# Decoder and gated cross attention on one core: mixing moved to the head of the step that begins another batch's scores, with new step lists for the products

## The chip, the cores and the metric

The kernel runs on one core of a Trainium2 chip. A core has five engines with queues of their own: TensorE (PE in the profile, its weight loads PEld), VectorE (DVE), ScalarE (ACT), GpSimd (POOL) and SyncE (SP), which here only issues DMAs. Each works through its instructions in order; semaphores hold an instruction until what it needs is there. The metric is the time of one execution in device microseconds (us). Lower is better.

## What is computed

Sixteen batches of 128 tokens with 512 features go through a decoder layer (self attention, cross attention, MLP) and then through a gated cross attention. All is float32. The reference, cut to what matters:

```python
# attention, 16 heads of 32
scores = einsum('bhqd,bhkd->bhqk', q, k) / sqrt(32)
scores = scores * mask - 10000.0 * (1.0 - mask)
probs = softmax(scores, axis=-1)
ctx = einsum('bhqk,bhkd->bhqd', probs, v)

# decoder layer
ln = layernorm(x, ln1_s, ln1_b)
q, k, v = split(ln @ w_qkv + b_qkv, 3)
x = x + merge_heads(attention(q, k, v, ltor_mask)) @ w_ao + b_ao
q = layernorm(x, ln2_s, ln2_b) @ w_q + b_q
k, v = split(ctx_2048 @ w_kv + b_kv, 2)
x = x + merge_heads(attention(q, k, v, cross_mask)) @ w_co + b_co
x = x + gelu(layernorm(x, ln3_s, ln3_b) @ w1 + b1) @ w2 + b2

# gated cross attention
a = layernorm(ctx_2048, ln_gamma, ln_beta)
Q, K, V = x @ Wq.T, a @ Wk.T, a @ Wv.T
out = x + tanh(gate) * (merge_heads(attention(Q, K, V, mask)) @ Wo.T)
```

## The kernel before

**Sections.** The sixteen batches form four groups of four. A *section* is the attention of one group: A0 to A3 (self attention), B0 to B3 (cross attention) and D0 to D3 (gated). `attend` (line 662) runs a list of sections twice: once the eight of the decoder, then, after the MLP, the four gated ones. Each call of it is a *run*. The MLP lies between the runs and is not touched.

**Steps.** A section has 16 steps, four for each batch. `step(k, ...)` (line 677) counts `k` on through the whole run, and `m = k % 4` is the place within a batch. The 16 heads of a batch are worked on as four *units* of four heads; a unit belongs to one step. What a unit goes through is spread over several steps: scaled (or, in D, masked with its least value found) on VectorE in the batch's first three steps (`SCALED`, line 658), exponentials on ScalarE a step later (`exp_unit`, four instructions), normalized on POOL after that (`norm_unit`, with a reciprocal of the sums on VectorE), turned by a 32x32 transpose on VectorE and sent to DRAM at `k - 3` (`turn_unit`, tiles `s` to `away`). Two units form a pair, which comes back from DRAM in four DMAs, with rows and columns of the big blocks exchanged (`receive_pair`, line 598, tile `pT`, three buffers).

**Scores and mixing.** At `m == 0`, `scores` (line 523) issues 16 small matmuls on the head's 32 rows (32x128 of the array, tile `sc`, four PSUM banks, which the next batch's scores use again). `mix` (line 609) multiplies the returned probabilities with the values: 16 small matmuls into 32 columns each (128x32 of the array, tile `av`). Its result is evicted by `mixed_out` on ScalarE into `mT` (one buffer), and `out_project` (line 644) makes four full matmuls of it (tile `mo`), whose sum goes to `x` on VectorE (`finish`). In the gated run the last product is put off: for D0 and D1 `put_away` sends `mT` to DRAM, for D2 it stays in SBUF, and these projections are done in D3 as block products (`added_product`, tile `mm_o`). The last batch of the gated run (`by_array`) is turned by TensorE instead of by DMA. Every matmul shows as two records in the trace.

**Where mixing stood.** In step `k`, batch `k // 4 - 2` was mixed at `m == 2`, that is at step `4b + 10` for batch `b`; its pairs were received at the head of steps `4b + 6` and `4b + 8`, and its output product came at `4b + 12`, at `m == 0`, after that step's jobs.

**Products.** While a section's attention runs, the projections of the next one are made between its steps. Most are block products with seven instead of eight quarter products (`block_product`, line 384, jobs 1 to 7, four matmuls each, eight records of 128x256). Jobs 1, 6 and 7 add up in the same PSUM bank `mm0`, which ScalarE copies out after each; 5 and 3 share `mm1` in the same way, with adds on VectorE; 2 and 4 take a bank of tag `pt` (two buffers), which `av` and `mo` also use. Which job comes in which step stands in lists written out by hand: `BLOCKS`, `SECOND_BLOCKS`, `CROSS_BLOCKS`, `GATED_BLOCKS` and `DEFERRED_BLOCKS` (lines 465 to 494); each is one dictionary per product, step to jobs. `blocks_plan` (line 496) joins them; without `as_listed` it puts jobs 1, 6 and 7 of a step first. The queries of B are made by whole chunks (`query_chunk`, 512 wide), not by blocks. The sums of operands that the blocks need are made on POOL in listed steps.

**Order in time.** The program's order of instructions on each engine is the order of issue. `afterwards` (line 79) puts something off to the call of `due` (line 82) in the next step, so that TensorE's result is there when ScalarE or VectorE comes to it. In a step the order is: receive a pair, scores, `due`, the jobs, output product, mixing, preparing the section after next (`ahead.prepare`), turning a unit, normalizing and exponentials, scaling.

## Time and profile before

| | |
|---|---|
| median of 3 runs | 1166.22 us (1162.94 to 1170.1) |
| profiled execution | 1168.78 us |
| its span, first to last instruction | 1167.0 us, 22047 instructions |
| mean granted TensorE clock | 0.994 |
| DMA | 259.80 MB, mean 223 GB/s |

The run of the decoder takes the first 560 us or so of the span, the MLP follows to 945, and the gated run takes the rest. A step of the A and B sections lasts 3.8 us on average: the scores of A2's first batch start at 162.82 us and those of A3's at 223.96, 16 steps later.

All instructions are recorded by one helper, so all carry its line, L50; they are told apart by engine and tile. `sc_A` are the scores of A, `av_B` the mixing of B, `mm_k_D` a key product of D. A row of the timeline gives start, busy time, engine, tiles, shape and count, and in brackets how long the engine had been idle before and what ended the wait. The costliest of the instructions that the change moves, or that stand beside them, by their mean durations:

| instruction | engine | ns |
|---|---|---|
| exponentials of one head block, 128x128, four a unit | ACT | 393 |
| normalizing a unit, 128x512 | POOL | 1041 |
| adding the mask in A, 128x512 | POOL | 1280 |
| mask and least value in D, 128x128, four a unit | DVE | 283 |
| eviction of `av` in A and B, 128x128, four a batch | ACT | 357 |
| eviction of `av` in D, 128x512 | ACT | 568 |
| scaling a unit in A, 128x512 | DVE | 681 |

### The profile page before, as it was taken

How to read it: one execution, taken by the hardware profiler on the slowest of the kernel's cores; microseconds unless marked ns; L12 is line 12 of the kernel's file. 1: busy time of each engine (PE TensorE's matmuls, PEld its weight loads, DVE VectorE, ACT ScalarE, POOL GpSimd, SP SyncE). 2: the span in 40 equal slices, each digit the busy share in tenths (PEclk: the TensorE clock that was granted, in tenths of full speed). 3: DMA queues.
4: the chain of work that ended last, by engine and by line, in shares of the span. 5: the costliest groups of instructions: out<-in, count | busy, mean ns of one | idle time of the engine just before them, and what ended most of it. 6: DMA issues, size and time to landing. Idle time of an engine off the chain costs nothing. (4 is left out here: it accounts for less than half of the span.)

```text
span 1167.0 us, 22047 instructions
## 1 busy us (share of the span) xinstructions
PE 1134.5 (97%) x7210; PEld 868.3 (74%) x7210; DVE 739.2 (63%) x1894; ACT 605.6 (52%) x2132; POOL 701.5 (60%) x636
## 2 busy tenths in 40 slices
PE   7999999999999999998999999999999999999988
PEld 5877777657575757545788888888888777878866
DVE  7678878797878877876663633543432247767753
ACT  2467667666666766674221333232222247867653
POOL 7698878688868776684333424433341367545973
PEclk9999999999999999999999999999999999999989
DMA  6598979999889879898796696696457728988964
GB/s 227 148 221 220 240 188 222 248 235 267 199 229 208 239 202 255 243 290 252 264 287 235 188 273 197 193 301 224 154 184 249 211 48 229 249 215 251 264 191 163
DMA packets 325266, 259.80 MB, mean 223 GB/s; under 512 B 83544, under 2 KB 280608, under 8 KB 320288
## 3 DMA queue, kind: packets, MB, share of 16 engines
q1 hardware_dynamic: 325112, 258.38, 78.0%
q8 instruction: 58, 0.95, 0.3%
q14 instruction: 56, 0.46, 0.1%
q10 hardware_dynamic: 40, 0.01, 0.0%
HBM read 163.94 MB, written 94.37 MB: 221 GB/s over the span
## 5 line engine op out<-in xcount | busy, mean ns | idle before, releaser
L50 ACT ACTIVATE s_A<-s_A,mn_A 128x128 f32<-128x128 f32 x256 | 99.5, 393 | 51.5 <-issue 37.3
L50 DVE TENSOR_TENSOR h<-h,h 128x512 f32<-128x512 f32 x80 | 54.9, 686 | 112.6 <-PE h L50 112.6
L50 ACT ACTIVATE s_B<-s_B,mn_B 128x128 f32<-128x128 f32 x256 | 99.5, 393 | 46.6 <-issue 32.5
L50 ACT ACTIVATE h<-h 128x512 f32<-128x512 f32 x64 | 40.3, 630 | 160.6 <-DVE h L50 160.6
L50 POOL TENSOR_TENSOR s_D<-s_D,sum_D 128x512 f32<-128x512 f32 x64 | 66.5, 1040 | 67.8 <-DVE sum_D L50 66.3
L50 ACT ACTIVATE s_D<-s_D,mn_D 128x128 f32<-128x128 f32 x256 | 99.2, 392 | 0.4 <-issue 0.4
L50 POOL TENSOR_TENSOR s_B<-s_B,sum_B 128x512 f32<-128x512 f32 x64 | 66.8, 1045 | 48.7 <-DVE sum_B L50 44.3
L50 POOL TENSOR_TENSOR s_A<-s_A,sum_A 128x512 f32<-128x512 f32 x64 | 66.6, 1041 | 36.0 <-DVE sum_A L50 35.3
L50 POOL TENSOR_TENSOR s_A<-s_A,ma 128x512 f32<-128x512 f32 x64 | 81.9, 1280 | 5.4 <-DVE s_A L50 3.7
L50 POOL TENSOR_TENSOR s_B<-s_B,mask 128x512 f32<-128x512 f32 x64 | 81.3, 1270 | 2.1 <-DMA away_B<-s_B 0.4
L50 POOL TENSOR_TENSOR rstd_aD<-rstd_aD,mhalf 128x1 f32<-128x1 f32 x12 | 6.6, 548 | 114.6 <-DVE rstd_aD L50 101.1
L50 POOL TENSOR_TENSOR sh<-h 128x512 f32<-128x512 f32 x32 | 40.7, 1272 | 50.9 <-ACT h L50 43.0
L50 PE MATMUL mo_B<-w_co,mT_B 128*128 128x512 f32 x128 | 60.5, 616 | 2.1 <-ACT mT_B L50 2.1
L50 PE MATMUL h<-T_C,t 128*128 128x256 f32 x256 | 60.7, 380 | 1.4 <-DVE h L50 1.4
L50 PE MATMUL h<-T_C,w 128*128 128x256 f32 x256 | 61.0, 381 | 0.8 <-DVE h L50 0.8
L50 PE MATMUL h<-sx,t 128*128 128x256 f32 x256 | 60.6, 380 | 0.0
L50 PE MATMUL o<-w,h 128*128 128x256 f32 x256 | 60.5, 379 | 0.0
L50 PE MATMUL o<-t,h 128*128 128x256 f32 x256 | 60.5, 379 | 0.0
L50 PE MATMUL o<-t,sh 128*128 128x256 f32 x256 | 60.5, 379 | 0.0
L50 PE MATMUL mo_A<-w_ao,mT_A 128*128 128x512 f32 x128 | 59.1, 604 | 0.0
L50 DVE CUSTOM_DVE_ANT_0 s_D<-sc_D,gmask 128x128 f32<-128x128 f32 x256 | 57.2, 283 | 0.9 <-DMA turned_x<-x_D 0.9
L50 PE MATMUL mm_q_B<-T_B,w_cq 128*128 128x512 f32 x128 | 57.3, 595 | 0.0
(324 smaller groups left out, 2986.1 us busy)
## 6 DMA issues: line engine op xcount, KB each, us to landing
t<-kept SPq DMA_DIRECT2D x24, 1024.0 KB, 6.9
away_A<-s_A SPq DMA_DIRECT2D x64, 256.0 KB, 3.0
pT_A<-away_A SPq DMA_DIRECT2D x128, 128.0 KB, 3.0
away_B<-s_B SPq DMA_DIRECT2D x64, 256.0 KB, 5.2
pT_B<-away_B SPq DMA_DIRECT2D x128, 128.0 KB, 3.6
away_D<-s_D SPq DMA_DIRECT2D x60, 256.0 KB, 3.7
pT_D<-away_D SPq DMA_DIRECT2D x120, 128.0 KB, 2.8
w<-in_L_xattn_w_dram SPq DMA_DIRECT2D x24, 512.0 KB, 5.6
```

The costliest lines, as they stand in the source:

```text
L50: return lambda *args, **kw: self.tc.keep_in_program_order(call(*args, **kw))
```

## The change

Mixing of batch `b` goes from step `4b + 10` to the head of step `4b + 12`, ahead of the scores of batch `b + 3`; its eviction is issued in the same step after `due`, and its output product (or the sending of `mT`) follows two steps after the mixing. The receives go two steps later too, to steps `4b + 8` and `4b + 10`, and now stand behind the scores in the step. Batches whose mixing would fall later than twelve steps before the scores of the run's last batch, that is behind the first step of the run's last section, keep their old steps (`k - 2`, `at - 2`), and the last batch of the gated run keeps its own. The lists of jobs are written anew, `blocks_plan` takes every list in the order in which it is written, B0 gets a list of its own (`FIRST_CROSS_BLOCKS`), the query chunks of B begin one step earlier, and the sums for B's value weights too.

```diff
--- before.py
+++ after.py
@@ -463,9 +463,9 @@
         return [[t[:, 2 * j : 2 * j + 2, i * HF : (i + 1) * HF] for j in range(2)] for i in range(2)]
 
     BLOCKS = (
-        {1: (1, 2), 2: (6,), 3: (7, 5), 5: (4,), 6: (3,)},
-        {5: (1,), 6: (2,), 7: (6,), 9: (7, 5), 10: (4,), 13: (3,)},
-        {10: (1,), 11: (6, 2), 13: (7,), 14: (5,), 15: (4, 3)},
+        {0: (1,), 1: (2, 6), 2: (5,), 3: (7, 4), 5: (3,)},
+        {4: (1,), 5: (2,), 7: (6, 5), 8: (7,), 9: (4,), 11: (3,)},
+        {9: (1,), 11: (2,), 12: (6,), 13: (5, 7), 15: (4, 3)},
     )
 
     FIRST_BLOCKS = (
@@ -474,31 +474,32 @@
     )
     SECOND_BLOCKS = (
         {4: (1, 2), 5: (6, 5), 6: (7, 4), 8: (3,)},
-        {7: (1, 2), 8: (6,), 9: (7, 5), 10: (4,), 11: (3,)},
-        {12: (1,), 13: (6, 2), 14: (7, 5), 15: (4, 3)},
+        {7: (1, 2), 8: (6,), 9: (5, 7), 10: (4,), 11: (3,)},
+        {10: (1,), 11: (2,), 12: (6,), 13: (5, 7), 15: (4, 3)},
     )
 
     CROSS_BLOCKS = (
-        {6: (1,), 7: (6, 2), 9: (7, 5), 10: (4,), 11: (3,)},
-        {11: (1,), 13: (6, 2), 14: (7, 5), 15: (4, 3)},
+        {4: (1,), 7: (2, 6), 8: (5,), 9: (7, 4), 11: (3,)},
+        {10: (1,), 11: (2,), 12: (6,), 13: (5, 7), 15: (4, 3)},
     )
+    FIRST_CROSS_BLOCKS = {6: (1,), 7: (2, 6), 8: (5,), 9: (7, 4), 11: (3,)}, CROSS_BLOCKS[1]
     GATED_BLOCKS = (
-        {0: (1,), 1: (2, 6), 2: (5, 7), 3: (4,), 5: (3,)},
-        {5: (1,), 6: (2, 6), 7: (7,), 8: (5,), 9: (4,), 10: (3,)},
-        {11: (1, 2), 12: (6,), 13: (5, 7), 14: (4,), 15: (3,)},
+        {0: (1,), 1: (2, 6), 2: (5,), 3: (7, 4), 5: (3,)},
+        {4: (1,), 5: (2,), 6: (6,), 7: (5, 7), 8: (4,), 9: (3,)},
+        {9: (1,), 10: (2,), 11: (6, 5), 13: (7, 4), 15: (3,)},
     )
     DEFERRED_BLOCKS = (
         {0: (1,), 1: (2, 6), 2: (5, 7), 3: (4,), 5: (3,)},
         {5: (1,), 6: (2, 6), 7: (5, 7), 8: (4,), 10: (3,)},
-        {12: (1,), 13: (2, 6), 14: (5, 7), 15: (4,), 17: (3,)},
+        {9: (1,), 11: (2, 6), 13: (5, 7), 15: (4,), 17: (3,)},
     )
 
-    def blocks_plan(products, blocks, as_listed=False):
+    def blocks_plan(products, blocks):
         out = {}
         for jobs, steps_ in zip(products, blocks):
             for step, ns in steps_.items():
-                out.setdefault(step, []).extend((not as_listed and n not in (1, 6, 7), jobs[n]) for n in ns)
-        return [([job for _, job in sorted(jobs, key=lambda j: j[0])], [step] * len(jobs)) for step, jobs in out.items()]
+                out.setdefault(step, []).extend(jobs[n] for n in ns)
+        return [(jobs, [step] * len(jobs)) for step, jobs in out.items()]
 
 
 
@@ -616,7 +617,8 @@
                     av[j * HD : (j + 1) * HD, c * S : (c + 1) * S], sec.v[:, b, h * HD : (h + 1) * HD],
                     bt.pT[j][:, :, c, :], start=True, stop=True,
                 )
-        mT = work.tile([P, KC, S], F32, tag="s", name=f"mT_{bt.name}", bufs=7) if bt.by_array else sec.mixed_tile(b)
+        at_end = work.tile([P, KC, S], F32, tag="s", name=f"mT_{bt.name}", bufs=7) if bt.by_array else None
+        mT = bt.mT = sec.mixed_tile(b) if at_end is None else at_end
 
         def mixed_out():
             if sec.v_bias is None:
@@ -627,8 +629,7 @@
                         mT[:, c], av[:, c * S : (c + 1) * S], AF.Identity, bias=col(sec.v_bias[0], sec.v_bias[1] + c)
                     )
 
-        afterwards("act", mixed_out)
-        bt.mT = mT
+        return mixed_out
 
     def out_project_last(bt):
 
@@ -670,40 +671,59 @@
         units, batches = [], []
         projected = deque()
 
+        last = (len(sections) * GB - 1) * GB
+
         def by_transfer(n):
 
-            return min(n, (len(sections) * GB - 1) * GB) if ready else n
+            return min(n, last) if ready else n
+
+        mixed_at, received_at = {}, {}
+        for b in range(len(sections) * GB):
+            k, at = (b + 3) * GB, (b + 2) * GB
+            if k > last - 3 * GB:
+                k, at = k - 2, at - 2
+            if ready and b * GB == last:
+                k = last + 7
+            else:
+                for half in range(2):
+                    received_at.setdefault(at + 2 * half, []).append(b * GB + 2 * half + 1)
+            mixed_at[k] = b
 
         def step(k, bt=None, jobs=(), ahead=None):
 
             m = k % GB
-            pair = k - 5
-            if pair % 2 and 0 <= pair < by_transfer(len(units)):
-                receive_pair(*units[pair])
+            pairs, done = received_at.get(k, []), mixed_at.get(k)
+            beside_scores = done is not None and m == 0
+            if beside_scores:
+                mixed_out = mix(batches[done])
             if m == 0 and bt is not None:
                 scores(bt)
+            for pair in pairs:
+                receive_pair(*units[pair])
             due()
+            if beside_scores:
+                mixed_out()
+                projected.append((k, batches[done]))
             for job in jobs:
                 job()
-            last_mix = ready and k == by_transfer(k) + 7
+            last_mix = ready and k == last + 7
             if last_mix:
-                mix(batches[-1])
-                projected.append(batches[-1])
-            if projected and (m == 0 or ready and bt is None):
-                before = projected.popleft()
+                afterwards("act", mix(batches[-1]))
+                projected.append((k, batches[-1]))
+            if projected and k - projected[0][0] >= (1 if ready and bt is None else 2):
+                before = projected.popleft()[1]
                 if before.by_array:
                     out_project_last(before)
                 elif before.sec.deferred:
                     afterwards("act", lambda: before.sec.put_away(before))
                 else:
                     out_project(before)
-            done = k // GB - 2
-            first_turned = ready and k == by_transfer(k) + 6
+            first_turned = ready and k == last + 6
             if first_turned:
                 turn_by_array(*units[k - 3])
-            if m == 2 and 0 <= done < len(batches) - ready:
-                mix(batches[done])
-                projected.append(batches[done])
+            if done is not None and not (beside_scores or last_mix):
+                afterwards("act", mix(batches[done]))
+                projected.append((k, batches[done]))
             if ahead is not None:
                 ahead.prepare(k % NS)
             if 0 <= k - 3 < len(units) and not first_turned:
@@ -727,8 +747,7 @@
 
         k = 0
         for i, sec in enumerate(sections):
-            last = i + 1 == len(sections)
-            jobs = others() if last else sections[i + 1].jobs()
+            jobs = others() if i + 1 == len(sections) else sections[i + 1].jobs()
             ahead = sections[i + 2] if i + 2 < len(sections) else after if i + 2 == len(sections) else None
             for b in range(GB):
                 bt = Batch(sec, b)
@@ -938,8 +957,8 @@
                 block_product(by_quarters(self.v), self.v_sides, token_sides, True, f"v_{n}"),
             ]
             return plan(
-                ([lambda c=c: self.query_chunk(c) for c in range(KC)], [1, 2, 3, 5]),
-                *blocks_plan(products, CROSS_BLOCKS), ([lambda: mask_terms(self.ms, self.ma)], [7]),
+                ([lambda c=c: self.query_chunk(c) for c in range(KC)], [0, 1, 3, 5]),
+                *blocks_plan(products, CROSS_BLOCKS if g else FIRST_CROSS_BLOCKS), ([lambda: mask_terms(self.ms, self.ma)], [7]),
                 ([lambda o=o: nc.gpsimd.tensor_tensor(*o) for o in sums], [0, 1, 2, 3]),
                 *(self.weights_begin() if g == 0 else decoder[NG + g - 1].tokens_again([5, 9, 13])),
             )
@@ -979,7 +998,7 @@
 
             return (
                 late_weights(), ([lambda n=n: k_sum(n) for n in range(4)], [4, 4, 5, 5]),
-                ([lambda n=n: v_sum(n) for n in range(4)], [9, 10, 11, 12]),
+                ([lambda n=n: v_sum(n) for n in range(4)], [8, 9, 10, 11]),
             )
 
         def scale_mask(self, s, sc, b):
@@ -1517,7 +1536,7 @@
             elif g == 3:
                 more = self.deferred_start()
             return plan(
-                *blocks_plan(products, GATED_BLOCKS, True), ([by_pool(o) for o in a_sums], [0, 1, 2, 3]), ([mask], [9]), *more
+                *blocks_plan(products, GATED_BLOCKS), ([by_pool(o) for o in a_sums], [0, 1, 2, 3]), ([mask], [9]), *more
             )
 
         def deferred_start(self):
@@ -1570,7 +1589,7 @@
             return (
                 ([lambda n=n: fetch_part("x0", x[0], n) for n in range(2, GB)], [1, 1]),
                 ([lambda g=g: add_later(g) for g in (1, 2) for _ in range(4)], [0, 1, 2, 3, 8, 9, 9, 10]),
-                *blocks_plan(later, DEFERRED_BLOCKS, True),
+                *blocks_plan(later, DEFERRED_BLOCKS),
                 ([lambda g=g, b=b: send(g, b) for g in range(3) for b in range(GB)], [8, 9, 10, 11, 13, 14, 15, 16, 19, 19, 19, 19]),
             )
```

## The prediction

> **What bounds the kernel now.** I read the page's busy table and clock row first, then the TensorE timeline, the waits, and the windows by section.
>
> ```profile
> PE 1134.5 (97%) x7210; PEld 868.3 (74%) x7210; DVE 739.2 (63%) x1894; ACT 605.6 (52%) x2132; POOL 701.5 (60%) x636
> PEclk9999999999999999999999999999999999999989
> ```
>
> TensorE is the bound: the others have a third or more of the span free. It is idle for 1167.0 - 1134.5 = 32.5 us, but busy time also hides lost time, so I took start-to-start times from its timeline (start, busy us, work):
>
> ```profile
> 385.75 3.62 PE L50 MATMUL mm_k_B<-x,w_ck 128*128 128x256 f32 x16
> 389.30 1.08 PE L50 MATMUL av_B<-pT_B,v_B 128*32 128x128 f32 x32
> 390.31 1.99 PE L50 MATMUL mm_v_B<-w_cv,T_e 128*128 128x256 f32 x8
> 392.14 1.89 PE L50 MATMUL mm_k_B<-T_e,sums_c 128*128 128x256 f32 x8
> 393.96 1.17 PE L50 MATMUL sc_B<-k_B,q_B 32*128 32x128 f32 x32
> 395.06 3.70 PE L50 MATMUL mo_B<-w_co,mT_B 128*128 128x512 f32 x8
> ```
>
> A block product (8 records of 128x256) in a run of its kind takes 1.73 us (400.32 to 402.05 in the same timeline). The two here take 1.83 (just after the mixing, av) and 1.82 (just before the scores, sc): each entry into small matmuls costs 0.10 us and each exit 0.10. A batch enters and leaves twice, for av and for sc.
>
> ```profile
> 1123.40 1.08 PE L50 MATMUL av_D<-pT_D,v_D 128*32 128x128 f32 x32
> 1124.41 0.49 PE L50 MATMUL sc_D<-k_D,q_D 32*128 32x128 f32 x4
> 1125.11 0.45 PE L50 MATMUL sc_D<-k_D,q_D 32*128 32x128 f32 x2 [0.21 <-DVE mn_D L50]
> 1128.72 2.04 PE L50 MATMUL sc_D<-k_D,q_D 32*128 32x128 f32 x26 [3.16 <-DVE mn_D L50]
> 1130.69 3.78 PE L50 MATMUL mm_o_D<-w_go,mT_D 128*128 128x256 f32 x8
> ```
>
> This is the only place where av is followed directly by sc: sc starts 1.01 us after av, as a full-array product does. It also shows the largest stall: the last batch's scores wait for VectorE to free their banks (6.28 us from 1124.41 to 1130.69 instead of the usual 1.10), and the next product then runs at half speed (3.58 us to its successor instead of 1.73).
>
> ```profile
> 1026.34 0.41 PE L50 MATMUL av_D<-pT_D,v_D 128*32 128x128 f32 x4
> 1029.48 1.92 PE L50 MATMUL av_D<-pT_D,v_D 128*32 128x128 f32 x28 [2.73 <-DMA pT_D<-away_D]
> 1031.33 3.99 PE L50 MATMUL mm_v_D<-w_gv,T_a 128*128 128x256 f32 x15
> ```
>
> Here the mixing waits for its transposed probabilities, which come back from DRAM. av takes 4.99 us instead of 1.01, and the product behind it 4.14 instead of 3.45: 4.67 us lost. The windows of the second and third gated section:
>
> ```profile
> 995.28:1046.61 51.33, 48.51 (x425) 39.87 (x424) 34.56 (x175) 37.30 (x153) 26.61 (x25) 0.97 0.90 239
> 1046.61:1092.91 46.30, 46.30 (x426) 38.44 (x425) 34.67 (x175) 33.98 (x150) 30.66 (x28) 1.00 0.88 248
> ```
>
> Same work, 5 us apart (first number length, second TensorE busy): D1 stalls, D2 does not.
>
> **The change part by part.** No instruction is added or removed; matmuls, evictions and DMAs keep their number.
>
> *Switches.* Mixing goes to the head of a step that opens with scores, for batches 0 to 25 of the decoder run and 0 to 9 of the gated run: 36. Each loses one exit and one entry: 0.107 + 0.096 = 0.203 us by the rows above, 36 x 0.203 = 7.3 us. Bounds: 0, if the drain only moves, to 7.3; I take 7.3, because the row at 1124.41 is the very sequence and shows no extra cost. [...]
>
> *Stalls in A and B.* At 153.56 and 214.69 a value product waits for VectorE's add of the key product 3 one step before, in the same bank (2.68 us instead of 1.73): 0.95 each. The new lists put 3 at step 11 and value 5 at 13, so both go: 1.9. At 250.09 and 436.39 product 6 waits for ScalarE's copy of product 1 from bank mm0 (1.2 each). With 1 at step 4 and 6 at 7 the second goes; in the first section of B, 1 stays at step 6 and the cover is product 2 (1.73) in place of av (1.0), so about 0.8 goes. Together 3.9, bounds 0 to 4.3. The moved jobs meet this: product 6 of A's queries comes at step 1 and needs POOL's second sum, done at 164.95 for a step 0 that begins at 162.82; TensorE reaches it 5.7 us into that section, so it is covered. ScalarE's eviction of av (four times 0.36) now stands at the step's head, behind it the copy of the step's product and four exponentials (1.56); the output product that needs it follows two steps later, 7 us, so it costs nothing.
>
> *Gated sections.* Stalls of D0 and D1, from start-to-start times: 965.93 0.84, 970.42 1.35, 978.46 1.02, 1016.44 0.49, 1026.34 4.67: 8.4 us. The receives of the probabilities go two steps later as the mixing does, so SP no longer waits for the send just before them. What is left is issue and landing:
>
> ```profile
> 1022.33 2.63 SPq L50 DMA_DIRECT2D pT_D<-away_D  x4
> pT_D<-away_D SPq DMA_DIRECT2D x120, 128.0 KB, 2.8
> ```
>
> Undisturbed, four issues take 1.75 us and land 2.8 later: 4.55. But the second pair is now asked for at the third step of a batch, and TensorE has only steps 2 and 3 until av: three products, 5.2 us, and at a section's end (steps 14 and 15) one product, 1.73, where before sc and three products (6.4) stood between. In A and B an output product stands there too: 6.9 or more, covered. In D the first three batches of a section just hold. At the end VectorE (mask 1.14, transpose 0.70 per unit) sets SP's time: transpose of step 13 about 4.0 us after step 12 begins, receive at 4.4, landed at 9.0, TensorE there at 7.5: a wait of 1.5 at three section ends, 4.5 us. ScalarE's exponentials and its group copies (0.8) end in time for the next scores, barely. Between no wait and 4.67 for each of ten batches I take 4.5, nearer to D2's row, which has none. One SP wait is new: the fetch of D1's kept mixing at step 11 stands in the same step as its last write (3.5 to land); the next receive is a step later with two steps to spare. Net 8.4 - 4.5 = 3.9.
>
> [...]
>
> *End.* The third deferred product set begins at step 9 instead of 12: products 1, 2 and 6 (3 x 1.73 = 5.2 us) now stand before the last batch's scores and fill its 5.18 us stall; the slow clock behind it (1.85 + 0.24) goes too: 7.3. In return two copies on ScalarE (0.58 each), an add on VectorE (0.69) and one on POOL (1.27) come into the chain that held those scores: I leave 1.5 as wait. After the scores TensorE had no gap until 1163.85, while VectorE waited 3.90 us and ScalarE 6.94 for it, so the others can follow a tail that is shorter by three products. Gain 5.8, bounds 0 to 7.3. The stalls at the end of the decoder run (523 to 552, some 9 us) stay: there the mixing is where it was.
>
> *Sum:* 7.3 + 3.9 + 3.9 + 5.8 = 20.9. The profiled execution took 1168.78 (span 1167.0); less 20.9 that is 1147.9. It lies 2.6 above the median 1166.22, from which the sum gives 1145.3. I say 1147.
>
> **The rivals.** *(a) The gated sections give back what they got:* each of their ten batches waits about 1.5 us instead of three, 15 us; net -6.6 there, gain 7.3 + 3.9 - 6.6 + 5.8 = 10.4, 1158. For: the cover fell from 8 to 10 us to 5.2; against: SP no longer waits for the sends (34.7 us of its waits). *(b) Slower:* the landing comes later than the cover in all ten gated batches, and each wait slows the clock as at 1026.34: 10 x 4.67 = 46.7 against 7.3 + 3.9 + 5.8 + 8.4 = 25.4, net +21, about 1189. It decides from 2.5 us per batch upward. For: DMA queues are 88 to 90% busy in D; against: landings there have a median of 2.8. *(c) It does not do what it says:* switching between the two small forms costs what it saves, and every filled stall comes back at the next bank; only the 3.9 of A and B remains, 1164.
>
> **How the numbers follow.** Forecast 0.66, (a) 0.16, (b) 0.09, (c) 0.09. A measurement of this kernel tells about 1% from no change: below 1154.6 is faster, above 1177.9 slower. (a) and (c) lie within 1%, except a fifth of (a): faster 0.69, same 0.22, slower 0.09. The forecast's best end is all stalls gone, 7.3 + 4.3 + 8.4 + 7.3 = 27.3, from the median 1139; I put the low end at 1138. Upward the range takes in (a) and most of (c): 1163.
>
> **What would show it.** Right: av followed by sc 1.01 us later in 36 places; A's sections at 59.4 instead of 61.1; no wait for DVE near the last scores; the tail after them near 26 us instead of 33. Wrong: waits of av_D for the DMA of pT_D over 4.5 us in total, or a new granted clock below 0.95 between 960 and 1120; waits of sc_D for DVE at the first step of a gated section.

## The result and the profile after

The changed kernel is a little slower: 1169.45 us against 1165.38 in the same comparison (22 runs of each), ratio 1.0033, 95% interval 1.0022 to 1.0043. A second comparison (run after_again) gave 1.0024, 1.0011 to 1.0036. The prediction said 1147 us, 1138 to 1163.

The page of the profiled execution (span 1167.4 us) looks like that of before; three microseconds less of busy TensorE, and slow clock in an earlier slice:

```profile
PE 1131.5 (97%) x7210; PEld 870.0 (75%) x7210; DVE 738.8 (63%) x1894; ACT 608.2 (52%) x2132; POOL 700.1 (60%) x636
PEclk9999999999999999999999999999999999999899
```

The TensorE timeline around the place shown before (start, busy us, work) now has the pair:

```profile
433.93 1.89 PE L50 MATMUL mm_k_B<-x,sums_c 128*128 128x256 f32 x8
435.75 1.08 PE L50 MATMUL av_B<-pT_B,v_B 128*32 128x128 f32 x32
436.76 1.17 PE L50 MATMUL sc_B<-k_B,q_B 32*128 32x128 f32 x32
437.87 1.99 PE L50 MATMUL mm_k_B<-x,w_ck 128*128 128x256 f32 x8
```

The scores start 1.01 us after the mixing, and there is one entry (433.93 to 435.75 is 1.82) and one exit (437.87 to 439.70 is 1.83). The pair stands so in 36 places, 27 of them at 1.01 or 1.02; in the other nine the mixing waits. The tail is as forecast too; the last scores (1135.75) wait for nobody:

```profile
1132.10 1.99 PE L50 MATMUL mm_o_D<-w_go,mT_D 128*128 128x256 f32 x8
1133.93 1.89 PE L50 MATMUL mm_o_D<-gsums_o,sums_mT 128*128 128x256 f32 x8
1135.75 1.17 PE L50 MATMUL sc_D<-k_D,q_D 32*128 32x128 f32 x32
1136.85 3.70 PE L50 MATMUL mo_D<-w_go,mT_D 128*128 128x512 f32 x8
```

So the saved switches and the shorter tail are there. Starts of scores in the two traces tell where they went:

| stretch | before | after | difference | forecast |
|---|---|---|---|---|
| to the first scores (A0) | 39.73 | 41.18 | +1.5 | 0 |
| A0 to the last decoder section (B3) | 433.39 | 427.07 | -6.3 | -9.2 (26 x 0.203, and 3.9) |
| B3, MLP, to D0 | 474.76 | 478.56 | +3.8 | 0 |
| D0 to D3 | 145.03 | 151.21 | +6.2 | -5.9 (10 x 0.203, and 3.9) |
| D3 to the end of the span | 74.1 | 69.4 | -4.7 | -5.8 |

**Start.** Sorting within a step was dropped, and the first lists feel it: in step 3 key product 1 (27.75) now comes after query product 3 (25.94), and its successor waits for ScalarE's copy.

```profile
25.94 1.97 PE L50 MATMUL mm_q_A<-T_A,sums 128*128 128x256 f32 x8
27.75 1.89 PE L50 MATMUL mm_k_A<-T_A,w_sk 128*128 128x256 f32 x8
30.66 1.53 PE L50 MATMUL mm_k_A<-sums_A,sums 128*128 128x256 f32 x6 [1.02 <-ACT k_A L50]
```

**A and B.** The four stalls of before lost 4.3 us. Three of them are gone; the fourth is not. In the first section of B product 6 of the keys (249.38) still waits for ScalarE's copy of product 1, and 1.02 us is lost there where it was 1.2. Five new stalls lose 2.7: two more around B0's keys (249.38 to 251.55 and 257.43 to 259.70: 0.44, 0.55), a product after scores at 421.71 (0.69), two mixings (451.86 and 466.79: 0.56, 0.45). Together 3.7.

**End of the decoder run.** From the mixing at 518.28 to the last one at 555.49 TensorE takes 37.21 us, 33.55 before (523.14 to 556.69):

```profile
522.36 5.40 PE L50 MATMUL mo_B<-w_co,mT_B 128*128 128x512 f32 x8 [2.44 <-ACT mT_B L50]
529.17 1.99 PE L50 MATMUL h<-T_C,w 128*128 128x256 f32 x8 [1.41 <-DVE x L50]
...
537.55 1.99 PE L50 MATMUL h<-T_C,t 128*128 128x256 f32 x8
542.20 5.40 PE L50 MATMUL mo_B<-w_co,mT_B 128*128 128x512 f32 x8 [2.65 <-ACT h L50]
```

The wait for `h` at 542.20 and that for `x` at 529.17 are new. An output product now shares a bank with the MLP's products: one mixing more (B2's second batch) falls into this section, after the rotation of `ps` (line 67) has been set, and shifts all later tiles by one place.

**Gated sections.** The windows of the second and third (first number length, second TensorE busy):

```profile
995.47:1043.90 48.43, 46.57 (x426) 39.01 (x424) 34.15 (x175) 37.47 (x152) 26.37 (x25) 1.00 0.93 241
1043.90:1098.02 54.12, 47.37 (x426) 39.67 (x424) 34.89 (x176) 33.30 (x149) 35.58 (x32) 0.95 0.86 230
```

D1 is 2.9 us shorter, D2 is 7.8 longer. Up to D3's first scores six mixings lose 11.2 us (1.60, 0.45, 1.30, 0.51, 0.34, 6.98) and products that wait for VectorE 5.7 (1.96, 1.16, 1.22, 1.40, each with the slower successor); before, all losses were 8.4. The largest, on TensorE and in SyncE's queue:

```profile
1088.11 1.99 PE L50 MATMUL mm_v_D<-gsums,T_a 128*128 128x256 f32 x8 [1.03 <-DVE v_D L50]
1090.03 0.41 PE L50 MATMUL av_D<-pT_D,v_D 128*32 128x128 f32 x4
1096.17 1.92 PE L50 MATMUL av_D<-pT_D,v_D 128*32 128x128 f32 x28 [5.72 <-DMA pT_D<-away_D]
1098.02 2.02 PE L50 MATMUL sc_D<-k_D,q_D 32*128 32x128 f32 x32
```

```profile
1078.04 0.52 SPq L50 DMA_DIRECT2D kept_mT_D<-mT_D  x1
1082.57 0.82 SPq L50 DMA_DIRECT2D mixed<-kept_mT_D  x2
1083.49 1.09 SPq L50 DMA_DIRECT2D away_D<-s_D  x1
1084.68 1.93 SPq L50 DMA_DIRECT2D pT_D<-away_D  x4
```

After the write at 1078.04 nothing is issued until 1082.57: the fetch reads what that write brings, and SyncE waits for its landing (3.9 us in the view of waits). This wait stands in the one queue that also carries the sends and receives: the receive that the mixing at 1090.03 needs begins at 1088.74, 6.49 us after the section's last scores (1082.25); one section earlier it was 3.28 (1034.78 to 1038.06).

The transfer itself also takes longer. From issue to landing the page gives 4.2 us (median), where it gave 2.8 before:

```profile
pT_D<-away_D SPq DMA_DIRECT2D x120, 128.0 KB, 4.2
```

The other runs below divide in the same way: 4.0 to 4.5 us in the nine traces with the late receives, 2.8 to 3.7 in the eleven with the early ones. What makes the landing longer isn't shown.

### The profile page after: what moved, and what is told of

Read it like the earlier page. It is cut to its first block, busy times and chain, and to the rows that moved or that the text cites. A ratio compares the mean times of both kernels' runs of the same rounds, so it can differ in the third digit from the quotient of the medians.

```text
span 1167.4 us, 22040 instructions
## 1 busy us (share of the span) xinstructions
PE 1131.5 (97%) x7210; PEld 870.0 (75%) x7210; DVE 738.8 (63%) x1894; ACT 608.2 (52%) x2132; POOL 700.1 (60%) x636
## 4 chain that ended last, share of the span: by engine, by line
PE 71%; DMA 8%; DVE 6%; POOL 6%; issue 4%; ACT 3%; SPq 2%; POOLq 0%; DVEq 0%; ACTq 0%
PE o L50 16%; PE h L50 16%; PE mo_B L50 4%; PE mm_v_B L50 4%; PE mm_k_A L50 4%; PE mo_A L50 4%; PE mm_q_B L50 3%; PE mm_k_B L50 3%; DMA pT_D<-away_D 3%; PE mm_q_A L50 3%; PE mm_v_A L50 2%; SPq L50 2%; PE mm_k_D L50 2%; PE mm_q_D L50 1%; POOL s_D L50 1%
## 5 line engine op out<-in xcount | busy, mean ns | idle before, releaser
L50 DVE CUSTOM_DVE_ANT_0 s_D<-sc_D,gmask 128x128 f32<-128x128 f32 x256 | 57.1, 283 | 11.2 <-PE sc_D L50 11.2
```

What stands on the lines that cost most here:

```text
L50: return lambda *args, **kw: self.tc.keep_in_program_order(call(*args, **kw))
```

## The experiments

All ratios are to the kernel before; one thousandth is 1.17 us.

**fetch_later**

```diff
-    for g in range(2) for n in range(KC)], [7, 7, 9, 9, 11, 11, 13, 13]),
+    for g in range(2) for n in range(KC)], [7, 7, 9, 9, 13, 13, 14, 14]),
```

> The changed kernel, with the fetch of D1's kept mixing moved from steps 11 and 13 of the third gated section to steps 13 and 14. In the changed kernel's trace SyncE stands 3.9 us at step 11 until the last write of that mixing has landed; behind it wait a send and two receives, and the last mixing of the section waits 5.72 us for its transposed probabilities (6.98 us lost there, 0.85 on the scores behind it). Theory 1 (the queue block makes this stall): the stall falls to the size of the same place one section earlier (0.51 lost at 1042.38), 7.3 us are regained, about 1162.1 where the changed kernel has 1169.45. Rival (the late receive makes it: two receives stand together at step 14 and land 3.7 us later whatever was before): the stall stays near 6 us, the time within 1 us of 1169.45. Second rival (another engine sets the end there, VectorE's transposes): half, about 1166.

Measured: 0.9964 (0.9948 to 0.998). Its timeline at the same mixing:

```profile
1088.94 0.41 PE L50 MATMUL av_D<-pT_D,v_D 128*32 128x128 f32 x4
1091.38 1.07 PE L50 MATMUL av_D<-pT_D,v_D 128*32 128x128 f32 x28 [2.02 <-DMA pT_D<-away_D]
1092.38 1.17 PE L50 MATMUL sc_D<-k_D,q_D 32*128 32x128 f32 x32
```

Of the 7.83 us lost at this mixing and its scores 2.43 are left: theory 1, with a remainder of 1.9 above the size that it named. The block was the largest single loss, 5.4 us by these rows. The other five mixings of the gated run still lose 3.7 together. The whole gained 7 to 8 us (0.9964 against 1.0033, or 1.0024 in after_again); what these rows don't account for is open.

**old_banks and banks_pt**

```diff
-        flip[0], in_blocks[0] = 2, False
+        flip[0], in_blocks[0] = 1, False
```

> The changed kernel, with the rotation of the four banks begun one place earlier in the last section of the decoder run, so that the mixings and output products at its end have the banks of before again (in the changed kernel one more of them falls into this section and shifts the rotation by one). Theory 1 (the shifted banks cost what was lost there): from the mixing at 518.28 to the last one 37.21 us become about 33.6 as before, 3.6 us regained, about 1165.8 where the changed kernel has 1169.45. Rival (other engines bound this stretch, so that arriving 4.9 us earlier only made TensorE wait longer): the stretch stays at 37, the time within 0.7 us of 1169.45.

Measured: 0.9995 (0.9976 to 1.0013). The stretch took 31.41 us, less than before the change, but the section's first mixing now took the bank `mm1` and waited 2.46 us for VectorE. The second edit, in place of the first, avoids that:

```diff
-        av = ps("mm", f"av_{bt.name}")
+        av = ps("pt" if bt.name == "B2_1" else "mm", f"av_{bt.name}")
```

> The changed kernel, with the extra mixing that falls into the last section of the decoder run (the second batch of B2) given a bank of the pair pt without advancing the rotation; every later mixing and output product then has the bank it has in the run old_banks, but the mixing itself no longer takes the bank mm1 in which the value product before it still waits for VectorE (2.46 us at 469.61 in old_banks). In old_banks the stretch from the mixing at 520.86 to the last one took 31.41 us, where the changed kernel takes 37.21 and the kernel before 33.55. Theory 1 (the shifted banks are the loss at the end of the decoder run): that stretch stays at 31.4, the wait of 2.46 is gone, 5.8 us regained on the changed kernel: 1.0033 of the time before becomes 0.998. Rival (waits there come and go with the phase of the DMAs): stretch back above 34, less than 3 us regained, 1.001 or more.

Measured: 0.9978 (0.9965 to 0.9991); the stretch took 32.45 us (517.20 to 549.65). The second output product, at 538.16, no longer waits; the first still does:

```profile
521.74 3.70 PE L50 MATMUL mo_B<-w_co,mT_B 128*128 128x512 f32 x8 [3.03 <-ACT mT_B L50]
525.27 1.89 PE L50 MATMUL h<-T_C,w 128*128 128x256 f32 x8
...
536.33 1.99 PE L50 MATMUL h<-T_C,t 128*128 128x256 f32 x8 [0.29 <-DVE h L50]
538.16 3.60 PE L50 MATMUL mo_B<-w_co,mT_B 128*128 128x512 f32 x8
```

4.8 us of the stretch, 5.5 thousandths (6.4 us) of the whole: the shifted banks are what was lost there, and 1.1 more than was lost.

**first_sorted** puts the old sort back for the first lists alone.

```diff
...
-                *blocks_plan(self.products(), FIRST_BLOCKS), prepare,
+                *blocks_plan(self.products(), FIRST_BLOCKS, True), prepare,
...
```

> The changed kernel, with the products of the first lists (before the first scores) put in the order of before again: those whose result ScalarE copies first within a step. Only one group of TensorE instructions changes place, four records of key product 1 before the query's product 5 at step 3. Theory 1 (this order lost the 1.45 us by which the changed kernel's first scores come later, 41.18 against 39.73): first scores at 39.7, and the lead is kept, 1168.0 where the changed kernel has 1169.45. Rival (the later start is a difference of these two executions' first DMA loads, or is taken up by the next wait): first scores at 41 or the gain gone by the second section, time within 0.5 us of 1169.45.

Measured: 1.0003 (0.9984 to 1.0021), first scores at 39.73, and key product 1 is followed without a wait (it stands before query product 3 again, which the expectation calls 5). The start is explained: over all twenty traces the first scores come at 39.28 to 40.27 us with the sort, but for one at 41.38 (best_put), and at 40.82 to 42.52 without. Whether the lead reaches the end is not settled: this trace's D0 begins at 948.00, later than the changed kernel's 946.81, and the interval overlaps with that of after_again.

**apart**

```diff
-            if beside_scores:
+            if beside_scores and ready:
                 mixed_out = mix(batches[done])
...
+            if not (beside_scores and ready):
+                for job in jobs:
+                    job()
             if beside_scores:
-                mixed_out()
+                (mixed_out if ready else mix(batches[done]))()
```

> The changed kernel, with the mixing of the decoder run put behind the products of its step again, so that 17 of its 26 adjacent mixings stand apart from the scores; its step, its receives and the lists stay. Theory 1 (each adjacent pair saves one exit and one entry, 0.203 us): 17 x 0.203 = 3.5 us slower, 1172.9 where the changed kernel has 1169.45, and entries and exits of 0.10 us around each mixing in A and B. [...] Rival two (the saving is taken up by waits elsewhere in the decoder run): no difference.

Measured: 1.0132 (1.0108 to 1.0156), far more than either theory. Where nothing else changed, the price can be read: A2 with four separated mixings took 60.51 us instead of 59.24; 0.48 of that is one wait, the other 0.79 is 4 x 0.20. Most of the rest is a new kind of stall; three in B lose 2.1 to 2.3 us each:

```profile
303.76 1.17 PE L50 MATMUL sc_B<-k_B,q_B 32*128 32x128 f32 x32
307.16 1.99 PE L50 MATMUL mm_k_B<-T_e,w_ck 128*128 128x256 f32 x8 [2.23 <-ACT q_B L50]
```

The key product takes the bank that the query chunk left, and with the mixing behind it ScalarE's copy is not done. So a mixing is also *cover* for the bank before it: work that keeps TensorE busy while another engine or a transfer finishes what TensorE needs next. The saving per pair is 0.20 us, as the row at 1124.41 of before said: between the two small forms no loss shows, the scores start 1.01 us after the mixing (436.76 after 435.75).

**tail_only** is the kernel before with one list of the change.

```diff
-        {12: (1,), 13: (2, 6), 14: (5, 7), 15: (4,), 17: (3,)},
+        {9: (1,), 11: (2, 6), 13: (5, 7), 15: (4,), 17: (3,)},
```

> The kernel before, with nothing of the change but the third list of deferred products (begun at step 9 instead of 12). My forecast gave this part 5.8 us (bounds 0 to 7.3): the 5.18 us of waiting at the last scores goes, the tail ends 5.8 earlier, 0.9950 of the time before. Theory from the changed kernel's trace (from the last section's first scores to the end 69.4 us there, 74.1 before, that is 4.7): 0.9960. Rival (other engines hold the end, and it was the later arrival that shortened the changed kernel's tail): 1.000.

Measured: 0.9951 (0.9934 to 0.9968), 5.7 us. This term of the sum holds by itself.

**gated_even and gated_old**

```diff
     GATED_BLOCKS = (
-        {0: (1,), 1: (2, 6), 2: (5,), 3: (7, 4), 5: (3,)},
-        {4: (1,), 5: (2,), 6: (6,), 7: (5, 7), 8: (4,), 9: (3,)},
-        {9: (1,), 10: (2,), 11: (6, 5), 13: (7, 4), 15: (3,)},
+        {0: (1,), 1: (2, 6), 2: (5,), 3: (7,), 4: (4,), 5: (3,)},
+        {5: (1,), 6: (2,), 7: (6,), 8: (5,), 9: (7,), 10: (4,), 11: (3,)},
+        {11: (1,), 12: (2, 6), 13: (5, 7), 14: (4,), 15: (3,)},
     )
```

> The changed kernel, with the 21 products of a gated section spread over its four batches as 5, 5, 5, 6 instead of 6, 6, 6, 3, and with product 4 between 7 and 3 in a step of its own at the end of each set. In the changed kernel value product 3 waits in three sections for VectorE (1.16, 1.22 and 1.40 us with the half-speed product behind it), key product 5 in the first section (1.96), and the mixing at the section ends 0.45, 0.51 and 6.98. Theory 1 (lists too thin before the section's end lose this): the 3.8 at products 3 and the 1.96 go, the mixings at section ends wait about the same, 5 to 6 us regained, 0.9985 of the time before. Rival (DVE's and SyncE's own chain sets the section's length, so the wait moves to the next mixing): less than 2 us regained, 1.002 or more.

Measured: 1.0069 (1.0047 to 1.009), 4 us worse than the changed kernel. Waits of TensorE between 946 and 1110 us (total, times, longest), here and in the changed kernel up to 1100:

```profile
PE av_D L50 <- DMA pT_D<-away_D: 11.4, 6, 4.0
PE mm_k_D L50 <- DVE k_D L50: 3.0, 2, 1.5
PE sc_D L50 <- DVE mn_D L50: 1.9, 1, 1.9
```

```profile
PE av_D L50 <- DMA pT_D<-away_D: 7.8, 3, 5.7
PE mm_v_D L50 <- DVE v_D L50: 2.7, 3, 1.0
PE mm_k_D L50 <- DVE q_D L50: 1.8, 1, 1.8
```

With one product fewer before each mixing in mid-section, those wait more (4.0 us at the longest): theory 1 falls. The rival's bound, 1.002 or more, holds, though it expected a small gain and not a loss. The product behind a wait for VectorE, which the expectation puts at half speed, was not: at 1088.11 of the changed kernel it took 1.92 us at a granted clock of 1.00. The cover between receive and mixing decides. gated_old has the lists of before, and

```diff
-            if k > last - 3 * GB:
+            if ready or k > last - 3 * GB:
                 k, at = k - 2, at - 2
```

> The changed kernel, with the gated run as before: its mixing and its receives two steps earlier, away from the scores, and its three lists; the decoder run and the deferred products stay as changed. Theory 1 (the gated part of the change lost 6.2 us between the first scores of that run and the last section, 151.2 us against 145.0): 6 us regained, 0.998 of the time before. Rival (the run starts with other DMA phases, and the stalls of the kernel before do not come back at their old size): section lengths between, 3 us regained. My forecast, had it been right, would make this 3.9 + 2.0 slower than the changed kernel, 1.008.

Measured: 0.9924 (0.9906 to 0.9943), faster than either theory had it. D1 and D2 take 47.70 and 46.40 us. Undoing the gated part alone regains 10.9 thousandths (12.7 us) on the changed kernel.

One reason that it regains more than the 6.2 us of the table lies in the trace of before. Its D0 to D3 took 145.03 us, and 142.63 to 142.90 in the three other traces with the gated run as before (tail_only, gated_old, best_old). The mixing that lost 4.67 us in D1 loses 1.2 to 1.5 in them; tail_only, whose code is unchanged up to D3:

```profile
1026.64 0.41 PE L50 MATMUL av_D<-pT_D,v_D 128*32 128x128 f32 x4
1028.15 1.07 PE L50 MATMUL av_D<-pT_D,v_D 128*32 128x128 f32 x28 [1.09 <-DMA pT_D<-away_D]
```

Against these three the change lost 7.5 to 8.6 us between D0 and D3 (150.43 in after_again, 151.21).

**early_receive, lists_old, early_lists_old** take that part to pieces; the third has both edits, the lists of before and:

```diff
                 k, at = k - 2, at - 2
+            elif ready:
+                at = at - 2
```

> The changed kernel, with the receives of the gated run's transposed probabilities two steps earlier, as before the change, while the mixing stays at the head of the step beside the scores. Between the run's first scores and its last section the changed kernel loses 12.0 us at mixings that wait for these transfers (1.60, 0.45, 1.30, 0.51, 0.34, 6.98, and 0.85 on the scores behind the last) and 6.0 at products that wait for VectorE (1.96 once, 1.2 to 1.4 three times). Theory 1 (the late receive is the larger loss): 9 to 10 of the 12.0 go, the 6.0 stay, 0.9955 of the time before. Rival (what holds SyncE's queue is the fetch of the kept mixing alone, and the wait for the sends comes back): at most the 5.4 us that the run fetch_later regained, 0.9985 or more.

> The changed kernel, with the three lists of products of a gated section as before the change; mixing, receives and all else as changed. The run gated_old, which also puts mixing and receives back, took 0.9924 of the time before, where the changed kernel takes 1.0033. Theory 1 (lists and receives each lose their own part): the 6.0 us at products that wait for VectorE go, the 12.0 at mixings stay within 3 us, 0.998 of the time before. Rival (the lists were made for the late mixing: with the old ones a mixing at a step's head has less work before it): the mixings wait longer, and the time is that of the changed kernel or more, 1.003 to 1.010.

> The changed kernel, with receives and lists of the gated run as before, only its mixing still at the head of the step beside the scores (two steps later than before). Theory 1 (the place of the mixing is not what loses; late receives and thin lists are): no mixing waits for its transfer more than 1 us, and the ten saved pairs of switches make it 2 us faster than gated_old (0.9924): 0.9907 of the time before. Rival (lists and place belong together, since the later mixing leaves its steps short of work elsewhere: product waits appear at the old lists): 0.994 or more.

| kernel | receives | lists | mixing | ratio | D0 to end, us |
|---|---|---|---|---|---|
| after (after_again) | late | new | beside scores | 1.0033 (1.0024) | 220.5 (219.8) |
| early_receive | early | new | beside scores | 0.9969 (0.9951 to 0.9986) | 213.4 |
| lists_old | late | old | beside scores | 1.0048 (1.0029 to 1.0066) | 223.6 |
| early_lists_old | early | old | beside scores | 0.9966 (0.9953 to 0.9979) | 212.9 |
| gated_old | early | old | as before | 0.9924 | 211.1 |

The late receive is the loss: 6.4 thousandths with the new lists, 8.2 with the old. With old lists and late receives mixings wait more (8.8 us in four places, 7.8 in the changed kernel). With early receives no mixing up to D3 waits for its transfer in either, as theory 1 of early_receive had it, and the lists make no difference; lists_old and early_lists_old both came out as their rivals. Of the two things that a late receive changes, the shorter cover and the longer landing, neither was tested alone. That is not all: beside the scores the gated mixing is still 1.8 us slower in the traces than in its old place, though it saves ten pairs of switches. In early_lists_old ScalarE and TensorE show why:

```profile
1001.95 0.59 ACT L50 COPY mT_D<-av_D 128x512 f32<-128x512 f32 x1 [2.65 <-DMA kept_mT_D<-mT_D]
1002.43 0.59 ACT L50 COPY q_D<-mm_q_D 128x512 f32<-128x512 f32 x1
```

```profile
997.47 3.72 PE L50 MATMUL mm_q_D<-T_D,w_gq 128*128 128x256 f32 x16
1003.16 1.97 PE L50 MATMUL mm_q_D<-x,gsums 128*128 128x256 f32 x8 [1.97 <-ACT q_D L50]
...
1017.64 1.89 PE L50 MATMUL mm_k_D<-gsums_a,gsums 128*128 128x256 f32 x8
1020.29 1.97 PE L50 MATMUL mm_k_D<-T_a,gsums 128*128 128x256 f32 x8 [0.77 <-ACT k_D L50]
```

The eviction waits until `mT`, one buffer, has been written away for the batch before; query product 1's copy stands behind it, and TensorE behind that. And key product 6 waits for the copy of 1, where before the mixing stood between them.

**put_sooner and two_mixed** both start from early_lists_old.

```diff
-            if projected and k - projected[0][0] >= (1 if ready and bt is None else 2):
+            if projected and k - projected[0][0] >= (1 if ready and (bt is None or projected[0][1].sec.deferred) else 2):
```

> early_lists_old, with the sending of each kept mixing (mT, one buffer) issued one step after the mixing instead of two. In early_lists_old ScalarE's eviction of a mixing waits 7.6 us in five places until the write of the batch before has landed (none in the kernel before, 1.8 in gated_old), and what stands behind it on ScalarE, the copy of query product 1 at 1002.43, holds TensorE 1.97 us. Theory 1 (this wait is what the mixing's new place costs in the gated run): the 7.6 fall below 2, the wait of 1.97 goes, some 3 us regained, 0.994 of the time before. Theory 2 (the cover that the mixing gave between two products of one bank is gone: key product 6 after 1 waits 0.77 in three sections): those three waits of 0.93 lost stay in any case. Rival (ScalarE had time, the products would wait anyway): 0.9966.

Measured: 0.9985 (0.997 to 0.9999). A miss: SyncE's queue was behind, the write left at 997.16 instead of 997.53, and the eviction still waited (10.0 us in all). two_mixed takes the wait away:

```diff
+            GatedAttention.second = masks[1][:, 1].rearrange("p o (c k) -> p (o c) k", k=S)
...
+            if self.g < 2 and b % 2:
+                return self.second
```

> early_lists_old, with a second buffer for the mixing's result in D0 and D1 (an unused half of a mask tile takes every other batch), so that ScalarE's eviction need not wait for the write of the batch before. Theory 1 (that wait, 7.6 us in five places, is what holds the products of the second section's start): no eviction waits for a write, the 2.25 us lost at 997.47 go, D1 takes 47.3 us instead of 49.27, and the time is 0.9946 of the time before (early_lists_old 0.9966). Theory 2 (the place also takes cover away): the three waits of key product 6 for ScalarE's copy of product 1 (0.93 lost each) stay. Rival (ScalarE is late for other reasons): 0.9966, D1 at 49.

Measured: 0.9963 (0.9947 to 0.9979).

```profile
996.90 3.72 PE L50 MATMUL mm_q_D<-T_D,w_gq 128*128 128x256 f32 x16
1000.46 1.89 PE L50 MATMUL mm_q_D<-x,gsums 128*128 128x256 f32 x8
```

No eviction waits for a write, query product 6 follows at once, and D1 takes 47.63 us, near the 47.3 expected. But the time stays: key product 6 still waits (1.51 and 0.93 lost), and in D2 a mixing waits 2.2 us for its transfer, 2.62 lost. The mechanism is shown at its place; its removal was given back later.

**Versions to beat both**

> The changed kernel with three parts undone: the gated run as before (as in gated_old, 0.9924), the banks at the end of the decoder run as in banks_pt (0.9978, that is 5.5 thousandths or 6.4 us less than the changed kernel's 1.0033), the first lists sorted as in first_sorted (first scores 1.45 us earlier). If the three are separate: 0.9924 - 0.0055 - 0.0012 = 0.9857. Rival (a lead gained earlier is taken up by waits for transfers later in the run, as part of first_sorted's was): half of the two smaller parts, 0.989.

> The changed kernel with its switches in the gated run kept (mixing beside the scores) but the receives two steps earlier (early_receive), the fetch of the kept mixing later (fetch_later), the banks of banks_pt and the sorted first lists. If keeping the ten adjacent mixings of the gated run is worth 10 x 0.203 us and the new lists lose 6.0: 4 us slower than best_old, 0.989 of the time before. Rival (with early receives the new lists lose nothing, their waits came from the mixings being late): 2 us faster than best_old, 0.984.

> best_old with the gated mixing beside the scores: old lists, receives two steps earlier, fetch of the kept mixing two steps later, banks as in banks_pt, first lists sorted. Theory 1 (the ten pairs of switches are saved there too): 2 us faster than best_old (0.9898), 0.988 of the time before. Rival: the time of best_old or more.

> best_old (0.9898) with the gated mixing beside the scores, receives and lists of the gated run as before, and the kept mixing sent one step after the mixing. If the saved switches (10 x 0.203) outweigh the three waits of 0.93 that come in: about 0.989, the same as best_old within what can be told. Rival (the eviction still waits): 0.992 or more, as best_beside had.

> The changed kernel itself, for the differences on this chip: 1.0033 of the time before by its first comparison. If a chip's own DMA times move the stalls, another ratio, and the parts' differences have to be read against that one.

Measured: best_old 0.9898 (0.9879 to 0.9917), 1155.03 us; best_early 0.9918 (0.9901 to 0.9935); best_beside 0.9928 (0.9911 to 0.9944); best_put 0.9926 (0.9899 to 0.9954); after_again 1.0024 (1.0011 to 1.0036). best_old came out at its rival's 0.989, so the parts don't add up in full; best_early is slower than both its numbers; best_beside and best_put came out as their rivals too, and in best_put's trace the eviction still waits for the write. best_old keeps the change in A and B and in the tail, and takes the gated run, the banks and the first order from before. Its clock row has no slow slice left:

```profile
span 1154.5 us, 22071 instructions
...
PEclk9999999999999999999999999999999999999999
```

## Why the prediction was wrong

The price of a switch and the tail came out as forecast; the sum missed by 21.3 us in the traces (20.9 forecast, 0.4 lost), most of it in the gated run. By its own terms:

- **Gated sections, net 3.9.** This step failed most: 8.5 us of stalls more instead of 3.9 fewer.
  - The largest single stall is the new wait of SyncE, which the sum put at nothing: "the next receive is a step later with two steps to spare". That counted steps of TensorE and not what stands between the fetch and the receive in SyncE's queue: the send of a unit, which the receive needs. It cost 5.4 us (fetch_later).
  - Products that wait for VectorE (5.7) were not priced at all.
  - "I take 4.5, nearer to D2's row" took the row with no wait as nearest, though that row had its receive two steps earlier. The term counted waits at three section ends; mid-section mixings waited too (1.60, 1.30). It also used a landing of 2.8 us, and with the late receives it was 4.2. With the fetch out of the way the mixings lose 6.2 (fetch_later), so here a size was off, and not by much. It priced the waits alone, with nothing slower behind them: the mixing's remaining 28 records did take 1.00 us after waits of 1.20 (985.47) and 2.02 us (fetch_later), but 1.85, at a clock of 0.50, after the 5.72.
  - The 8.4 us to be regained came from one execution. By the three other traces of the old gated run some 2 us of it was chance.
- **Switches, 7.3.** The price of 0.203 a pair held (A2; apart). The "drain" of its bounds is a name for this loss; what TensorE does in that time no trace shows. What failed is that the mixing was looked at as cover only in A and B ("the cover is product 2 in place of av"): in the gated run its going made key product 6 wait for the copy of 1, and the ten pairs brought nothing (early_lists_old against gated_old).
- **Stalls in A and B, 3.9.** Mis-sized: 4.3 lost before and 3.7 after, 0.6 net; the lead at B3 was 6.3 instead of 9.2. In B0 "about 0.8 goes" was 0.2: TensorE has 5.2 us of work between products 1 and 6 there, but ScalarE does four exponentials and a query copy first and ends the copy of product 1 only at 249.29.
- **End, 5.8.** Right: 5.7 alone (tail_only), 4.7 in the changed kernel.
- "**The stalls at the end of the decoder run** (523 to 552, some 9 us) stay: there the mixing is where it was." Wrong by 3.7: the place was the same, the bank was not (banks_pt).
- **The start** was left out. Dropping the sort changes every list, and the first lists were not compared: 1.5 us.

Rival (a) came nearest for the gated run, with 6.6 us more of stalls, but not by its own way: six batches waited and not ten, 11.2 us and not 15, half of it behind the fetch, and the 5.7 at VectorE were not in it. Alone it would have given 1158. Banks, start and the new stalls of A and B did the rest. Not settled is why gated_old beats early_lists_old by 4.2 thousandths (4.9 us), when the traces differ by 1.8 from D0 on.

## What to carry to other kernels

When a step is moved, list for each engine and queue what stood behind it and what it stood between: a small matmul between two products of one bank was cover here (without it a key product waited 0.77 us in early_lists_old, 2.23 in apart), and a rotation of buffers is part of every later instruction (4.8 us of a stretch, by banks_pt). A transfer asked for later has to be set against the work left on the bounding engine before its use, unit by unit, with all that stands ahead of it in the queue. A stall read off one execution may be smaller in the next (4.67 us in before, 1.2 to 1.5 in three other traces); look at a second trace before counting on it. Test the parts of such a change one by one: here two were worth 5 to 6 us each (the tail; A and B, by best_old against tail_only), and one, the gated run, cost 13.

## What the runs showed of the hardware

In these runs the granted clock did not follow the length of one wait. Windows of the changed kernel and of banks_pt (length, TensorE busy; the third number from the end is the granted clock) hold the same output product, after 2.44 and after 3.03 us of waiting:

```profile
522.36:529.17 6.81, 5.40 (x9) 2.03 (x9) 3.01 (x8) 3.63 (x15) 6.65 (x7) 0.75 1.01 302
```

```profile
521.74:525.27 3.53, 3.53 (x8) 1.62 (x9) 0.91 (x3) 3.06 (x12) 3.45 (x4) 1.00 1.05 309
```

The shorter wait was followed by 0.75, the longer by 1.00. Waits for the same kind of output product in other runs are as mixed: after 2.12 (before) and 2.23 us (apart) it took 5.2 and 5.4, after 2.30 (old_banks) 3.7. Waits of small matmuls in the trace of before, 2.73 us (until 1029.48) and 3.16 us (until 1128.72), were followed by a granted clock of 0.50. How long TensorE can wait without a slower clock behind it can't be told from these rows.

Programs with the same decoder run differ from execution to execution: D0's first scores came between 945.55 and 949.37 us in ten traces of nine such kernels. A difference of 3 us between single traces that lies before the edit says nothing.
